# A differential-attention and mixture-of-experts kernel: set-up in a written order, q spread one piece to a round, and the second norm's statistics taken from the first's

## Chip, core and metric

The kernel runs on one core of a Trainium2 chip. The metric is the device time of one execution in microseconds (us). Several executions are timed, and the median counts. A profiled execution has a time of its own, and beside it a span, which goes from the first to the last instruction of the core.

## What is computed

The input x has 8 sequences of 512 tokens with 128 features. Each sequence goes through differential attention with 16 heads of 8 features, a residual and a layer norm, then through a mixture of 8 experts of which each token uses 2, again with a residual and a layer norm.

```python
q, k1, k2, v = (heads(x @ W.T) for W in (Wq, Wk1, Wk2, Wv))
a1 = softmax(causal(q @ k1.T * SCALE))
a2 = softmax(causal(q @ k2.T * SCALE))
attn = a1 - sigmoid(lambda_logit) * a2
attn = attn / max(sum(abs(attn), -1), 1e-6)
x = layernorm(x + (attn @ v) @ Wo.T)

# the experts
xn = (x - mean(x)) * rsqrt(var(x) + EPS) * gamma + beta
probs = softmax(xn @ router_w.T / 1.5)
w, idx = top_k(probs, 2)
y = sum over the two chosen e of w[e] * (silu(xn @ W1[e]) @ W2[e])
x = layernorm(y + x)
```

The first layer norm has no gain and no offset. The experts' own norm, which is called the second norm here, is taken of the first norm's result. All is in float32, with EPS = 1e-5 in each of the three norms.

## The kernel before

**Tiles.** A sequence is worked in 16 units `Unit(b, j)` of 32 queries. A unit holds the scores of 4 heads times 32 queries on the 128 partitions, for 4 groups of heads and 2 softmaxes. Unit j looks at L = 32 (j + 1) keys, so units grow along a sequence. The first 8 units are worked in 2 slots, the last 8 in 4 slots.

**Rounds.** One slot gives one round (`round_of`, from line 1122). All five engines work in the order in which a round writes its instructions (`manual_schedule`, line 1180); nothing reorders them later. A round does, in this order: the products with v of a unit that is ready (line 529, tile po); the next slot's scores on PE (line 366, tile sc, and the mask's product on line 375 from i4 and mk); copies of transposed weights on ACT (line 512, aT); steps that wait in `on_act`; the negated maxima on DVE (lines 388 and 396, nm); the transposes of an earlier piece on PE (line 487, pt); steps that wait in `on_dve`; the combination of the two softmaxes, which is on DVE a sum (line 432, junk) and on POOL the scaling of the second softmax (line 442, et); and the exponentials on ACT (line 406, et). After that it takes one task from each of several queues:

- `misc`: the tasks of a block of 128 tokens (`block_tasks`) and of the next sequence's projections (`projection_tasks`). One task is taken per round.
- `routing`: the choice of experts for a chunk of blocks.
- `moves` and `gathers`: indirect DMAs on POOL's queue (lines 811 and 959), which send rows to the tiles of the experts and fetch results. One is taken per round.
- `experts`: tiles of expert work, at a pace that is worked out when a chunk has been routed.

A task often puts its DVE part into `on_dve`, and that part runs in the next round.

**Blocks.** The tasks of a block are `reciprocals`, `normalise`, `project_out`, `first_norm`, `second_norm`, `turn` and `logits`. The DVE part of `project_out` adds the residual (xa, line 590), takes its statistics (`stats_of`, lines 118 and 119) and has POOL raise the variance to the power -1/2 (`rstd_of`: l_ve on DVE at line 110, l_rs on POOL at line 112). `first_norm` writes x1 (line 600), takes the statistics of x1 in the same way and has POOL work out a second power. `second_norm` writes xh (line 615). There are 32 blocks, so 64 pairs of statistics for these two norms; the last layer norm has another 32.

**Projections.** `project_q` multiplies on PE; its part `spread` copies the result to qs on DVE (line 299) and writes four pieces of qb on POOL one after the other (line 301), each with another column of hms, which selects heads. k goes through ACT to kT (line 315). v goes through DVE to vt (line 323), and 8 DMAs on SP copy parts of it to vr (line 327), which the products with v read for short rows of keys.

**Set-up.** Lines 59 to 275 and the projections of sequence 0 (line 1079) stand outside `manual_schedule`. There the framework's scheduler orders the instructions of each engine. It put slam1 (line 226), i4 and mk (lines 218 and 219) ahead of the copy of the first x (line 292) on DVE; the memsets of all constants first on POOL; and the four fills of the row buffers with zero (line 271) ahead of the copies to vr on SP. ACT issues the loads of wq, wv, slam, gam, bet and rw, and works out slam with a sigmoid (line 225).

The first four chunks (6, 9, 9 and 6 blocks) go to experts by rows that are sent; the last 2 blocks go through all 8 experts.

Of the kernel before, what the change touches and what calls it, by code (L numbers as in the profile page):

```python
# [20 lines left out]
def kernel(  # L21
# [43 lines left out]
    nhalf = const.tile([P, CB], F32, name="nhalf")  # L65
    nc.gpsimd.memset(nhalf, -0.5)
    rank = const.tile([P, CB, E], F32, name="rank")
    for e in range(E):
        nc.gpsimd.memset(rank[:, :, e : e + 1], float(E - e))

# [4 lines left out]
    before = const.tile([P, P], BF16, name="before")  # L75
    nc.gpsimd.memset(before, 1.0)
    nc.gpsimd.affine_select(
        out=before,
        in_=before,
        pattern=[[1, P]],  # L80
        compare_op=ALU.is_ge,
        fill=0.0,
        base=-1,
        channel_multiplier=-1,
    )
    ones = const.tile([P, P], BF16, name="ones")
    nc.gpsimd.memset(ones, 1.0)

    upto = const.tile([P, E, E], F32, name="upto")
    for e in range(E):  # L90
        nc.gpsimd.memset(upto[:, e, : e + 1], 1.0)
        if e + 1 < E:
            nc.gpsimd.memset(upto[:, e, e + 1 :], 0.0)

    fill = const.tile([P, E, CB], F32, name="fill")
    for k in range(CB):
        nc.gpsimd.memset(fill[:, :, k : k + 1], float(P * k))

    def tiles_of(nb):

        return (2 * nb * P + E * (P - 1)) // P

    number = const.tile([P, tiles_of(CB), E], F32, name="number")
    for t in range(tiles_of(CB)):
        nc.gpsimd.memset(number[:, t, :], float(t))

# [27 lines left out]
    with ExitStack() as actx:  # L134
# [52 lines left out]
        for h in range(4):  # L187
            nc.scalar.dma_start(
                slam[Q * h : Q * h + Q, :],
                lam.rearrange("(g h) -> h g", h=4)[h].partition_broadcast(Q),  # L190
            )
        for g in range(NG):
# [3 lines left out]
            )  # L196
        nc.scalar.dma_start(gam, gamma.unsqueeze(1))
        nc.scalar.dma_start(bet, beta.unsqueeze(1))
        nc.scalar.dma_start(rw_sb, rw)


        nc.gpsimd.memset(hsel, 1.0)
        for low in (True, False):
# [9 lines left out]
            )  # L213
        nc.vector.tensor_reduce(hm, hsel, AX.X, ALU.max)
        nc.vector.tensor_scalar_mul(hms, hm, SCALE)
        for g in range(NG):
            r = slice(32 * g, 32 * g + 32)
            nc.vector.tensor_copy(i4[r], identb[r, r].unsqueeze(1).to_broadcast([32, 4, Q]))
            nc.vector.tensor_copy(mk[r], maskb[r, r])
        nc.vector.tensor_copy(wq_sb.rearrange("p (a b d) -> p a b d", a=NP, b=2), wqp[:, :, :, 0:HD])  # L220
        for s in range(2):
            nc.vector.tensor_copy(
                wk_sb[:, s].rearrange("p (a b d) -> p a b d", a=NP, b=2), wkp[:, :, :, s, 0:HD]
            )
        nc.scalar.activation(slam, slam, AF.Sigmoid)
        nc.vector.tensor_scalar(slam1, slam, 1.0, None, ALU.add)
        for h in range(4):
            nc.vector.tensor_scalar_mul(wo_sb[:, h, :], won, hm[:, h : h + 1])


# [29 lines left out]
        zero = aw.tile([P, D], F32, name="zero")  # L260
        nc.gpsimd.memset(zero, 0.0)
        chunks, n0 = [], 0
# [3 lines left out]
        for n0 in range(n0, NB, 2):  # L266
            chunks.append(Chunk(n0, 2, False))

        for c in chunks:
            if c.sparse:  # L270
                nc.sync.dma_start(
                    c.xs.rearrange("(t p) d -> p t d", p=P),
                    zero.unsqueeze(1).to_broadcast([P, c.nt, D]),
                )
        chunk_of = {n: c for c in chunks for n in range(c.n0, c.n0 + c.nb)}

        def projection_tasks(b):
# [16 lines left out]
            def project_q():  # L294
                pm = ps_m.tile([P, T], F32, tag="pm", name=f"pmq_{b}")
                nc.tensor.matmul(pm, lhsT=wq_sb, rhs=xTf, start=True, stop=True)

                def spread():
                    nc.vector.tensor_copy(qs, pm)
                    for h in range(4):  # L300
                        nc.gpsimd.tensor_scalar(  # L301
                            qb[:, :, h, :],
                            qs.rearrange("p (j q) -> p j q", q=Q),
                            hms[:, h : h + 1],
                            1.0,
                            ALU.mult,
                            ALU.mult,
                        )

                on_dve.append(spread)  # L310
# [226 lines left out]
        def block_tasks(b, i, blk):  # L537
# [39 lines left out]
            def project_out():  # L577
# [10 lines left out]
                def residual():  # L588
                    xa = bp.tile([P, D], F32, tag="xa", name=f"xa_{n}")
                    nc.vector.tensor_add(xa, pm, xts[b][:, i, :])  # L590
                    mv = bp.tile([P, 1, 2], F32, tag="mv1", name=f"mv1_{n}")
                    stats_of(bp, xa, mv[:, 0, :], "l1")
                    s["xa"], s["mv"], s["rs"] = xa, mv, rstd_of(bp, mv, 1, "l1")

                on_dve.append(residual)

            def first_norm():
                def norm():
                    x1 = s["x1"] = ch.x1[:, ci, :]
                    nc.vector.tensor_scalar(  # L600
                        x1, s["xa"], s["mv"][:, 0, 0:1], s["rs"], ALU.subtract, ALU.mult
                    )
                    mv = bp.tile([P, 1, 2], F32, tag="mv2", name=f"mv2_{n}")
                    stats_of(bp, x1, mv[:, 0, :], "l2")
                    s["mv2"], s["rs2"] = mv, rstd_of(bp, mv, 1, "l2")

                on_dve.append(norm)

            def second_norm():
                def norm():  # L610
                    if ch.sparse:
                        s["xh"] = ch.xh[:, ci, :]
                    else:
                        s["xh"] = bp.tile([P, D], F32, tag="xh", name=f"xh_{n}")
                    nc.vector.tensor_scalar(
                        s["xh"], s["x1"], s["mv2"][:, 0, 0:1], s["rs2"], ALU.subtract, ALU.mult
                    )

                on_dve.append(norm)
# [16 lines left out]

            return [reciprocals, normalise, project_out, first_norm, second_norm, turn, logits]

# [428 lines left out]

        on_act, on_dve, on_dve_late = [], [], []

# [3 lines left out]
        def run(steps):  # L1073
            now = list(steps)
            steps.clear()
            for step in now:
                step()

        for task in projection_tasks(0):
            task()  # L1080
            run(on_dve)
            run(on_act)

# [38 lines left out]
        def round_of(now=None, ahead=None):  # L1122
# [40 lines left out]
            for _ in range(1 if now else 2):  # L1163
                if moves:
                    moves.popleft()()
                elif gathers and (now or not misc and not routing):
                    gathers.popleft()()
# [12 lines left out]
        with tc.manual_schedule(  # L1180
# [6 lines left out]
            }  # L1187
        ):
            last = None
            for b in range(B):  # L1190
# [21 lines left out]
            while (  # L1212
                to_combine or to_transpose or to_evacuate or to_multiply
                or misc or routing or experts or moves or gathers or on_act or on_dve or on_dve_late
            ):
                round_of()
# [49 lines left out]
```

## Time and profile before

| | |
|---|---|
| Time of three runs | 1224.34, 1222.89 and 1214.82 us, median 1222.89 us |
| Profiled execution | 1229.11 us, span 1227.1 us |
| Mean granted clock of TensorE | 0.923 |
| Busy share of the span | PE 90%, DVE 77%, ACT 64%, POOL 44% |
| First scores on PE | 20.03 us after the span's start |
| Last scores on PE | about 1105 us |

PE is TensorE's matmul, PEld its loading of weights, DVE VectorE, ACT ScalarE, POOL GpSimd and SP SyncE, which here only issues DMAs. Times in the profile's rows count from the span's start, and line numbers are those of the kernel before. A row of the timeline gives start, duration, engine, line, operation, the tile written and the tile read, the shape, the count, and in brackets the idle time of the engine ahead of it with what ended it. A row of the chain of waits gives start, duration and what the chain went through at that time. The row that begins with PEclk shows the clock that TensorE was granted in 40 equal parts of the span, in tenths of full speed.

### The profile page before, as it was taken

The numbers are of one execution on the slowest core, as the hardware profiler recorded it, in microseconds if no ns is written. First come the engines' busy times: TensorE is split into PE (matmuls) and PEld (weight loads), VectorE is DVE, ScalarE is ACT, GpSimd is POOL, SyncE is SP. The second block draws the span as 40 slices with busy tenths as digits, with TensorE's granted clock in tenths as the row PEclk, the third lists the DMA queues.
The fourth block names the chain that finished last, engine by engine and source line by source line (L and its number), as shares of the span: only waits on it lengthen the run. The fifth ranks groups of instructions, "written<-read, shape, count | busy, mean of one in ns | idle before, by whom it ended". The sixth has DMA issues, their size and how long they took to land.

```text
span 1227.1 us, 28291 instructions
## 1 busy us (share of the span) xinstructions
PE 1101.6 (90%) x9450; PEld 779.6 (64%) x9450; DVE 948.4 (77%) x2900; ACT 782.7 (64%) x2776; POOL 543.0 (44%) x967
## 2 busy tenths in 40 slices
PE   4999899888999899989898899988899889997786
PEld 2556555555666666666566666665667667776675
DVE  4688778867888678887689888879767897975656
ACT  4578767557777667766576777776567665763221
POOL 4343434464433343356556442343643762364333
PEclk8699969878999789997899999999989998999998
DMA  8000000011121111110133113221222333435762
GB/s 245 7 8 1 10 2 8 26 59 30 30 82 45 33 42 53 46 41 23 38 99 85 57 45 91 63 56 47 72 78 72 105 107 105 126 92 149 215 188 68
DMA packets 128897, 84.30 MB, mean 69 GB/s; under 512 B 22896, under 2 KB 114288, under 8 KB 128752
## 3 DMA queue, kind: packets, MB, share of 16 engines
q1 hardware_dynamic: 110944, 68.25, 19.8%
q0 software_dynamic: 3840, 7.87, 2.3%
q10 hardware_dynamic: 13968, 6.37, 1.8%
q8 instruction: 76, 1.25, 0.4%
q14 instruction: 69, 0.57, 0.1%
HBM read 63.31 MB, written 17.56 MB: 66 GB/s over the span
## 4 chain that ended last, share of the span: by engine, by line
PE 56%; DVE 19%; ACT 10%; issue 6%; POOL 4%; DMA 4%; ACTq 0%; SPq 0%; POOLq 0%; DVEq 0%
PE pt L487 18%; PE sc L366 12%; ACT et L406 6%; PE po L529 5%; PE sc_None L366 5%; PE pa L914 5%; PE pz L934 4%; DVE junk L432 3%; DVE nm L396 3%; DVE nm L388 2%; PE pmo L580 2%; ACT aT L512 2%; DVE l_st L118 1%; DMA got<-ys,row 1%; POOL qb L301 1%
## 5 line engine op out<-in xcount | busy, mean ns | idle before, releaser
L442 POOL TENSOR_SCALAR et<-et,c 128x224 f32<-128x224 f32 (+15 forms) x512 | 266.9, 526 | 438.6 <-DVE junk L432 301.2
L487 PE MATMUL pt<-ident,et 128*128 128x128 f32 (+1 forms) x2048 | 330.0, 297 | 36.6 <-POOL et L442 20.7
L406 ACT ACTIVATE et<-sc,nm 128x512 f32<-128x512 f32 (+7 forms) x512 | 299.7, 593 | 68.8 <-DVE nm L396 46.8
L487 PEld LDWEIGHTS pt<-ident,et 128*128 128x128 f32 (+1 forms) x2048 | 231.9, 146 | 171.6 <-issue 59.9
L396 DVE TENSOR_REDUCE nm<-sc 128x2 f32<-128x576 f32 (+7 forms) x256 | 251.6, 983 | 41.8 <-PE sc L375 41.5
L432 DVE SCALAR_TENSOR_TENSOR junk<-et,c 128x224 f32<-128x224 f32 (+15 forms) x512 | 264.2, 516 | 9.6
L512 ACT COPY aT<-pt 128x384 f32<-128x384 f32 (+5 forms) x488 | 185.8, 407 | 130.5 <-PE pt L487 127.4
L366 PE MATMUL sc<-kT,qb 32*128 32x384 f32 (+7 forms) x1024 | 246.5, 558 | 13.3 <-ACT et L406 12.4
L406 ACT ACTIVATE et<-sc_None,nm 128x256 f32<-128x256 f32 (+7 forms) x512 | 188.1, 385 | 31.2 <-DVE nm L388 23.2
L366 PE MATMUL sc_None<-kT,qb 32*128 32x512 f32 (+7 forms) x512 | 118.6, 546 | 22.3 <-ACT et L406 21.1
L388 DVE TENSOR_REDUCE nm<-sc_None 128x4 f32<-128x256 f32 (+7 forms) x128 | 96.0, 751 | 40.8 <-PE sc_None L375 40.5
L366 PEld LDWEIGHTS sc<-kT,qb 32*128 32x128 f32 x1024 | 78.4, 187 | 63.7 <-ACT et L406 30.6
L112 POOL TENSOR_TENSOR l_rs<-l_ve,nhalf 128x1 f32<-128x1 f32 x96 | 62.5, 651 | 124.9 <-DVE l_ve L110 102.8
L934 PE MATMUL pz<-xgT,w 128*128 128x128 f32 x704 | 101.5, 291 | 11.4 <-DVE xgT L908 10.7
L406 ACT ACTIVATION_READ_ACCUMULATOR et<-sc_None,nm 128x1 f32 x512 | 107.4, 210 | 0.0
L406 ACT ACTIVATION_READ_ACCUMULATOR et<-sc,nm 128x1 f32 x512 | 103.2, 202 | 0.0
L934 PEld LDWEIGHTS pz<-xgT,w 128*128 128x128 f32 x704 | 92.0, 203 | 16.7 <-DVE xgT L908 13.5
L914 PE MATMUL pa<-w,hT 128*128 128x128 f32 x704 | 100.0, 289 | 0.6 <-ACT ysb L924 0.6
L914 PEld LDWEIGHTS pa<-w,hT 128*128 128x128 f32 x704 | 93.2, 206 | 1.9 <-issue 1.2
L879 ACT ACTIVATE th<-pz 128x512 f32<-128x512 f32 x88 | 52.7, 599 | 58.3 <-PE pz L934 52.1
L529 PE MATMUL po<-aT,vt 128*32 128x128 f32 (+1 forms) x2048 | 85.2, 291 | 0.0
L811 POOL DMA_INDIRECT xs<-xh,row x60 | 65.4, 1089 | 42.9 <-DMA xs<-xh,row 30.8
(148 smaller groups left out, 1316.2 us busy)
## 6 DMA issues: line engine op xcount, KB each, us to landing
w<-in_w_dram SPq DMA_DIRECT2D x192, 256.0 KB, 3.0
xg<-xs SPq DMA_DIRECT2D x88, 64.0 KB, 3.3
ys<-ysb ACTq DMA_DIRECT2D x88, 64.0 KB, 1.5
xs<-zero SPq DMA_DIRECT2D x2, 1600.0 KB, 13.8
xs<-zero SPq DMA_DIRECT2D x2, 1216.0 KB
xt<-in_x_dram SPq DMA_DIRECT2D x8, 256.0 KB
out_dram<-ot SPq DMA_DIRECT2D x32, 64.0 KB, 2.1
vr<-vt SPq DMA_DIRECT2D x32, 32.0 KB, 1.9
```

The costliest lines, as they stand in the source:

```text
L366: nc.tensor.matmul(parts[gi][:, :, :L], lhsT=qb[r, j].rearrange("p h q -> p (h q)"), rhs=kT[r, sets, :L], start=True, stop=False,)
L388: nc.vector.tensor_reduce(self.nm[:, g, :], sc.rearrange("p g (s l) -> p g s l", s=2)[:, :, :, : self.L], AX.X, ALU.max, negate=True,)
L396: nc.vector.tensor_reduce(self.nm[:, g, s], sc[:, :, : self.L], AX.X, ALU.max, negate=True)
L406: nc.scalar.activation(self.et[:, g, si, : self.L], sc[:, gi, lo : lo + self.L], AF.Exp, bias=self.nm[:, g, si : si + 1], accum_out=self.b ...
L432: nc.vector.scalar_tensor_tensor(junk[:, :L], self.et[:, g, 1, :L], self.c2[:, g : g + 1], self.et[:, g, 0, :L], ALU.mult, ALU.max, accum_ ...
L442: nc.gpsimd.tensor_scalar(self.et[:, g, 1, :L], self.et[:, g, 1, :L], self.c2[:, g : g + 1], -1.0, ALU.mult, ALU.mult,)
L487: nc.tensor.matmul(pt[: len(gs) * kw, x_, :], lhsT=lhsT, rhs=ident, is_transpose=True, start=(k == 0), stop=(k == 1),)
L512: nc.scalar.copy(self.aT[: rows[done], self.used + done : self.used + end, :], pt[: rows[done], done:end, :],)
L529: nc.tensor.matmul(self.blk["po"][32 * g : 32 * g + 32, self.jj, :], lhsT=v[:rows, kb, 32 * g : 32 * g + 32], rhs=self.aT[:rows, self.at[g ...
L811: nc.gpsimd.indirect_dma_start(ch.xs[:, :], bass.IndirectOffsetOnAxis(ap=ch.row[:, k, c : c + 1], axis=0), ch.xh[:, c, :], None,)
L914: nc.tensor.matmul(pm[:, 1, :], lhsT=hT[y][:, f, :], rhs=w[y][1][:, f, :], start=(f == 0), stop=(f == NF - 1),)
L934: nc.tensor.matmul(pz[:, f, :], lhsT=w[t][0][:, f * P : (f + 1) * P], rhs=xgT[t], start=True, stop=True,)
```

## The change

**Set-up.** The projections of sequence 0 and the set-up steps that are no load now stand inside `manual_schedule`, in a written order: first x's transposes and their copy, then hm and hms, then the other projections with the spreads of q, then i4 and mk, slam, slam1 and wo_sb, then the constants on POOL, and at the end the four zero fills. The loads of slam, gam, bet and rw go from ACT to SP. The sigmoid is worked out as 0.5 (tanh(x / 2) + 1), with the tanh on ACT.

**Spreads.** The four pieces of qb go into a queue `on_pool`, and a round takes one of them, in place of a task of `moves` or `gathers`. In set-up all four run at once.

**Second norm.** With v the variance of the residual sum, the first norm's result has mean 0 and variance v / (v + EPS). So the second norm of it is the residual sum, less its mean, times ((1 + EPS) v + EPS²)^(-1/2). `norms` takes the place of `first_norm` and `second_norm`: both powers come from one POOL instruction on two columns, and xh and x1 are written from xa in one step.

```diff
+                    ve = bp.tile([P, 2], F32, tag="l1_ve", name=f"l1_ve_{n}")
+                    nc.vector.tensor_scalar(ve[:, 0:1], mv[:, 0, 1:2], EPS, None, ALU.add)
+                    nc.vector.tensor_scalar(
+                        ve[:, 1:2], mv[:, 0, 1:2], 1.0 + EPS, EPS * EPS, ALU.mult, ALU.add
+                    )
+                    rs = bp.tile([P, 2], F32, tag="l1_rs", name=f"l1_rs_{n}")
+                    nc.gpsimd.tensor_tensor(rs, ve, nhalf[:, :2], ALU.pow)
...
-            def first_norm():
+            def norms():
                 def norm():
-                    x1 = s["x1"] = ch.x1[:, ci, :]
-                    nc.vector.tensor_scalar(
-                        x1, s["xa"], s["mv"][:, 0, 0:1], s["rs"], ALU.subtract, ALU.mult
-                    )
-                    mv = bp.tile([P, 1, 2], F32, tag="mv2", name=f"mv2_{n}")
-                    stats_of(bp, x1, mv[:, 0, :], "l2")
-                    s["mv2"], s["rs2"] = mv, rstd_of(bp, mv, 1, "l2")
-
-                on_dve.append(norm)
-
-            def second_norm():
-                def norm():
+                    x1 = ch.x1[:, ci, :]
...
-                    nc.vector.tensor_scalar(
-                        s["xh"], s["x1"], s["mv2"][:, 0, 0:1], s["rs2"], ALU.subtract, ALU.mult
-                    )
+                    for k, dst in enumerate((s["xh"], x1)):
+                        nc.vector.tensor_scalar(
+                            dst,
+                            s["xa"],
+                            s["mv"][:, 0, 0:1],
+                            s["rs"][:, 1 - k : 2 - k],
+                            ALU.subtract,
+                            ALU.mult,
+                        )
...
                 def spread():
                     nc.vector.tensor_copy(qs, pm)
-                    for h in range(4):
...
+                    on_pool.extend(lambda h=h: spread_head(h) for h in range(4))
...
             for _ in range(1 if now else 2):
-                if moves:
+                if on_pool:
+                    on_pool.popleft()()
+                elif moves:
                     moves.popleft()()
...
+            first = projection_tasks(0)
+            first.pop(0)()
+            run(on_dve)
+            nc.vector.tensor_reduce(hm, hsel, AX.X, ALU.max)
+            nc.vector.tensor_scalar_mul(hms, hm, SCALE)
+            for task in first:
+                task()
+                run(on_dve)
+                run(on_act)
+                run(on_pool)
+
+            for g in range(NG):
+                r = slice(32 * g, 32 * g + 32)
+                nc.vector.tensor_copy(i4[r], identb[r, r].unsqueeze(1).to_broadcast([32, 4, Q]))
+                nc.vector.tensor_copy(mk[r], maskb[r, r])
+
+            nc.scalar.activation(slam, slam, AF.Tanh, scale=0.5)
+            nc.vector.tensor_scalar(slam, slam, 1.0, 0.5, ALU.add, ALU.mult)
+            nc.vector.tensor_scalar(slam1, slam, 1.0, None, ALU.add)
+            for h in range(4):
+                nc.vector.tensor_scalar_mul(wo_sb[:, h, :], won, hm[:, h : h + 1])
+            nc.gpsimd.memset(zero, 0.0)
+            for e in range(E):
+                nc.gpsimd.memset(rank[:, :, e : e + 1], float(E - e))
...
+            for c in chunks:
+                if c.sparse:
+                    nc.sync.dma_start(
+                        c.xs.rearrange("(t p) d -> p t d", p=P),
+                        zero.unsqueeze(1).to_broadcast([P, c.nt, D]),
+                    )
```

## The prediction

> **What bounds the kernel now.** I read the page first: busy shares, the clock row, the chain that ended last.
>
> ```profile
> PE 1101.6 (90%) x9450; PEld 779.6 (64%) x9450; DVE 948.4 (77%) x2900; ACT 782.7 (64%) x2776; POOL 543.0 (44%) x967
> PEclk8699969878999789997899999999989998999998
> PE 56%; DVE 19%; ACT 10%; issue 6%; POOL 4%; DMA 4%; ACTq 0%; SPq 0%; POOLq 0%; DVEq 0%
> ```
>
> No engine is the bound alone. The chain changes between PE, DVE and ACT within every round, because a round hands a score tile from PE to DVE to ACT to DVE to POOL and back to PE. So an instruction that goes is worth what stood on the chain, not its busy time. In the clock row the digits 6 to 8 are stretches at half clock. Next I read the start in the chain of waits (start us, duration us, what):
>
> ```profile
> 7.22 3.20 DMA slam<-in_lam_dram
> 10.49 1.28 ACT L225
> 12.03 0.17 DVE slam L226
> ...
> 13.63 0.70 DVE xT L292
> ...
> 17.28 2.71 POOL qb L301 x4
> ...
> 20.54 0.30 DVE nm L388
> 20.86 3.17 ACT et L406 x22
> 24.03 7.56 DMA vr<-vt
> 31.63 1.21 PE po L529 x8
> ```
>
> Two detours are to be seen. DVE copied xT only at 13.63, behind slam's load and sigmoid and eight small copies, although its input pmx was there at 6.78 (5.69 + 1.09, timeline). And the first po waited until 31.63 for vr, whose DMAs stood on SP behind four zero fills; PE was idle 2.1 us for it (group row of po<-aT,vr: 2.1 <-DMA vr<-vt).
>
> Then the timeline where POOL spreads q of the next sequence, four in a row (start, duration, engine, what, idle before):
>
> ```profile
> 72.32 0.61 DVE L422 TENSOR_TENSOR c<-c,r 128x4 f32<-128x4 f32 x1
> 72.96 0.93 DVE L432 SCALAR_TENSOR_TENSOR junk<-et,c 128x288 f32<-128x288 f32 x1
> 74.56 0.86 DVE L432 SCALAR_TENSOR_TENSOR junk<-et,c 128x288 f32<-128x288 f32 x1
> 76.09 0.50 DVE L432 SCALAR_TENSOR_TENSOR junk<-et,c 128x288 f32<-128x288 f32 x1
> 72.23 2.89 POOL L301 TENSOR_SCALAR qb<-qs,hms 128x512 f32<-128x512 f32 x4 [0.62 <-DVE c L418]
> 75.85 0.55 PE L487 MATMUL pt<-ident,et 128*128 128x128 f32 x3 [1.20 <-POOL et L442]
> ```
>
> While POOL spreads, et waits behind it and PE stands 1.20 us. And DVE's operations with two tensors are longer: junk 0.93 and 0.86 against 0.50 right after, c 0.61 against 0.16.
>
> **Part 1, set-up order.** I lay the after order on the old times. wk lands at 7.20 and its two copies end at 7.59 as before; xT is then first on DVE, at 7.6 instead of 13.63, 6.0 us sooner, with hm and hms after it (0.34, beside PE's q product). From xT's start to the last spread it took 6.35 us (13.63 to 19.98) and to the end of the vt copy 6.76 (20.39). So qb is there at about 13.95 and vt at 14.4. But what was ahead of xT now stands between vt and the first nm: eight i4 and mk copies (0.78 + 0.70), two on slam (2 x 0.17), four wo_sb (0.88), 2.7 us. The first nm starts at 17.1 instead of 20.54: 3.4 us gained. Bounds: 0 (a load is late) and 6.0 (nothing of the 2.7 counts).
>
> Loads: SP now issues xt and wk (0.45 + 0.49), slam (4 x 0.39), won (4 x 0.64), gam, bet and rw (0.44 + 0.46 + 0.34), 7 us in all. One of won's waits for wk's landing (7.20), so SP is through at about 10; slam, at 3.2 us to landing, is there by 7 to 10, won by 12. They are needed at 13.3 (tanh behind kT's copies) and 16.2 (wo_sb). If won came 2 us later than 16.2, those 2 us would be lost. ACT's second table load (1.28 us from 19.32) ended at 20.60, before nm was done at 20.84: nothing. On POOL the constants' memsets (2.9 us, 1.82 to 4.84 without the mask, and zero) go behind the spreads, 13.95 to 16.9; et is first wanted at 24.00 - 3.4 = 20.6, so 3.7 us of cover.
>
> vr: eight issues at 0.62 us (median of the line) from 14.4 end at 19.4, and 1.9 us to landing gives 21.3; po will want it at 29.5 (end of the pt before it) - 3.4 = 26.1. The stall of 2.1 us goes (bounds 0 and 2.1). The zero fills, 14.75 us of issue, follow until about 34 and hold up only xt of sequence 1 on SP, wanted at 68.74; the filled rows are first written at 230.4.
>
> Part 1 sums to 5.5 us.
>
> **Part 2, spreads.** The same seven spreads outside set-up (28 instructions) stay; they stand one to a round, behind that round's et. PE's waits for et behind the bursts, read at each of the seven: 1.20, 1.19, 0.30, 0, 3.53, 0, 0.99, together 7.2 us. Against it: DVE's stretched operations stay possible. Per burst they cost 0.45 + 0.43 + 0.36 = 1.24 us, 8.7 over seven. A spread of 0.69 that starts behind an et of 0.50 ends 1.19 us after the junk that released it; DVE's nm between takes 0.81, so the next junk can lose 0.38, four times a sequence: 28 x 0.4 = 11 us. Gain 7.2 + 8.7 - 11 = 4.9 if all counts, minus 2.5 if PE's waits are filled otherwise, 11.2 if nothing is lost (the spreads' own time on the chain between 60 and 1110, summed from its pieces). I take 4, near the first, as other waits are known to come up behind. The scatters wait up to four rounds behind spreads; the two built programs have the same PE work after the last scores (375 instructions in both), so this moves nothing into the tail.
>
> On this the Trainium skill speaks against the change: "SBUF — State Buffer", section "Who interferes with whom", says that VectorE with two SBUF inputs and a GpSimd instruction reading SBUF exclude each other, the later one waiting until the first ends. The rows above (0.93 for 0.50) fit. By the rule's full wait of one 0.69 spread each, 28 x 0.69 = 19 us would be lost and part 2 would cost 3 us; by the row it gains 4.
>
> **Part 3, norms.** One block, from the timeline:
>
> ```profile
> 60.65 0.33 DVE L600 TENSOR_SCALAR x<-xa,mv,l_rs 128x128 f32<-128x128 f32 x1
> 61.02 0.29 DVE L118 BATCH_NORM_STATS2 l_st<-x 128x6 f32<-128x128 f32 x1
> 61.35 0.18 DVE L119 BATCH_NORM_AGGREGATE mv<-l_st 128x2 f32<-128x6 f32 x1
> 61.56 0.15 DVE L110 TENSOR_SCALAR l_ve<-mv 128x1 f32<-128x1 f32 x1
> 61.80 0.69 POOL L112 TENSOR_TENSOR l_rs<-l_ve,nhalf 128x1 f32<-128x1 f32 x1 [1.47 <-DVE l_ve L110]
> ```
>
> The second statistics go: 0.29 + 0.18 of DVE and one pow on POOL for each of 32 blocks. l_ve stays twice (the second moves into the first round), both normalisations stay but share a round. With the gaps that is (0.33 + 0.21) = 0.54 us, 17 us of DVE at most. x of line 600 stands on the chain for 16 of 32 blocks, so 16 x 0.5 = 8 us stood there; behind it another engine is soon late (ACT 64% and PE 90% busy), so I take 5, bounds 0 and 17. The pow with two columns has no row; one column takes 0.547 to 0.947 here, so two cost between that and double, which is no more than the two pows of before. POOL loses up to 32 x 0.57 = 18 us of work, and l_rs is on the chain for 1.8 us between 60 and 1110: 1 us. Every block's logits come one round sooner; the last block's end at 1139 while the sparse tiles keep PE until 1183, so that hides it.
>
> **Sum.** 5.5 + 4 + 5 + 1 = 15.5 us. The profiled execution took 1229.1 (span 1227.1 and 2.0 around it), giving 1213.6; it lies 6.2 above the median of 1222.9. Taken off the median: 1207.4. The chance bounds are 1% of the median, 1210.7 and 1235.1, about what a measurement here can tell from no change.
>
> **Rivals.**
> *Only the start counts.* DVE and POOL savings hide behind PE (90% busy), as POOL's 302 us of waiting for junk suggests; against it stand the measured PE waits behind the bursts. 1222.9 - 5.5 = 1217.4.
>
> *The clock helps too.* The first half-clock stretch lasts from about 24.5 to 55; PE was fully busy from 32, after the vr wait, and got the clock back some 21 us later. Another stretch (152 to 176) also lasts 20.5 us at full business. If the count starts anew at an idle gap, removing the wait ends the stretch some 5 to 10 us sooner, 3 to 5 us of work; with part 3 at 10: 1207.4 - 4 - 5 = 1198. The Trainium skill's "TensorE: Matmul & The Clock Gate", section "What's actually happening", has the clock return after about 3.4 us of business; the trace's 21 us contradicts it, and by the rule nothing would come on top.
>
> *The clock hurts (slower).* At the start of sequences the matmuls are short and PE falls to half clock:
>
> ```profile
> 152.00:176.00 24.00, 23.00 (x125) 13.43 (x126) 16.90 (x62) 16.30 (x72) 8.27 (x19) 0.57 0.00 1
> 690.00:714.00 24.00, 20.77 (x183) 14.30 (x181) 21.53 (x78) 18.72 (x80) 10.46 (x23) 1.00 0.20 58
> ```
>
> The column after POOL is the clock. DVE did 16.9 us of work in 24 instead of 26.1 in 30 at full clock (60 to 90), so such a stretch costs 24 - 16.9 x 30 / 26.1 = 4.6 us. The starts of later sequences, as at 690, escape it now. To end over 1% slower it needs (12.2 + 15.5) / 4.6 = 6 new stretches; with seven, 1207.4 + 32 = 1240. For it: a one-round shift moves every boundary. Against: late sequences are filled with expert matmuls.
>
> **How the numbers follow.** Forecast 0.50, only the start 0.27, clock helps 0.15, clock hurts 0.08. About 0.45 of the forecast's 0.50 lies below 1210.7: faster 0.45 + 0.15 = 0.60; slower 0.08; the rest 0.32 within 1%. Low is 1222.9 - (8.1 + 11 + 9) = 1195; high is 1222.9 - 2.1 = 1221, which leaves out the clock rival and the ends of the first.
>
> **What would show it.** First nm near 17 us; no DMA wait ahead of the first po; waits of pt for et above 1 us after spreads gone; DVE busy near 933 (948.4 less 32 x 0.477); 64 pows; same number of half-clock stretches. It is wrong if nm starts after 20, if junk beside spreads grows by more than 11 us in all, or if PE's share on the chain takes over all that DVE gives up.

## The result, and the profile after

The changed kernel takes 1217.05 us (median of 20 runs), the kernel before in the same runs 1224.12 us: ratio 0.9932, 95% interval 0.9908 to 0.9956. The gain is 7 us, less than half of the 15.5 that were forecast; the time lies in the stated range. Its profiled execution took 1212.04 us, with a span of 1210.1 and a mean granted clock of 0.927.

The page after (busy shares, clock row, chain):

```profile
PE 1093.9 (90%) x9450; PEld 776.2 (64%) x9450; DVE 927.1 (77%) x2837; ACT 780.4 (64%) x2775; POOL 526.8 (44%) x935
PEclk7699969797999999989998999997899799998998
PE 60%; DVE 16%; ACT 11%; issue 6%; POOL 4%; DMA 3%; ACTq 1%; POOLq 0%; SPq 0%; DVEq 0%
```

DVE lost 21.3 us of work and POOL 16.2, and the chain moved from DVE (19% to 16%) to PE (56% to 60%).

The chain of waits at the start:

```profile
7.64 0.61 DVE xT L251
...
14.38 0.70 DVE vt L284
15.16 1.95 DMA vr<-vt
17.11 0.08 issue
17.19 0.19 DVE i L1165
...
18.18 0.88 DVE wo_sb L1172 x4
19.06 0.21 DVE nm L349
...
28.27 0.59 PE po L490 x8
```

xT stands at 7.64, as forecast, and no DMA stands right ahead of po. (The row that names vr's DMA from 15.16 covers time in which DVE stood in two copies, as the next rows show.) But nm starts at 18.97 (timeline; 17.1 forecast). DVE's timeline shows what took the difference:

```profile
14.38 0.69 DVE L284 COPY vt<-pmv 128x512 f32<-128x512 f32 x1 [3.28 <-PE pmv L281]
14.99 1.85 DVE L1165 COPY i<-identb 32x128 bf16<-32x128 bf16 x1
15.09 1.76 DVE L1166 COPY mk<-maskb 32x32 bf16<-32x32 bf16 x1
16.89 0.18 DVE L1165 COPY i<-identb 32x128 bf16<-32x128 bf16 x1
```

The first pair of copies took ten times as long as the others. POOL's memsets of the constants ran from 13.86 to 16.79, one after the other; the copies end when they do.

POOL at the first spreads outside set-up, in the timeline:

```profile
71.21 0.51 POOL L403 TENSOR_SCALAR et<-et,c 128x288 f32<-128x288 f32 x1 [1.05 <-DVE junk L393]
71.70 0.97 POOL L258 TENSOR_SCALAR qb<-qs,hms 128x512 f32<-128x512 f32 x1
72.64 0.50 POOL L403 TENSOR_SCALAR et<-et,c 128x288 f32<-128x288 f32 x1
73.12 0.69 POOL L258 TENSOR_SCALAR qb<-qs,hms 128x512 f32<-128x512 f32 x1
```

Each spread stands behind an et. PE's waits of pt for et fell from 20.7 to 9.7 us (first line before, second after, from PE's waits: total, times, longest):

```profile
PE pt L487 <- POOL et L442: 20.7, 24, 3.5
```

```profile
PE pt L448 <- POOL et L403: 9.7, 17, 1.6
```

So all three parts do in the profile what they should, and yet more than half of the forecast gain is missing.

**The clock.** Runs of one and the same kernel spread widely (those of the kernel before by 29 us within one set of runs, 1211.4 to 1240.4), and the spread follows the mean granted clock of each run: over 199 runs (the kernel before and the first twelve experiments) a run with 0.01 less clock takes 6.6 us more. So each kernel below has three numbers: its median; its mean clock less that of the kernel before; and its difference *at equal clock*, from straight lines of time over clock with a common slope (5.6 to 8.0 us per 0.01, by the set) and an offset for each kernel. The last is an adjustment, since the clock was not set by hand, but it splits what a part saves from what it does to the clock. A clock difference from 12 runs is known to 0.004 or 0.005. Runs more than 1.5% above their kernel's fastest are left out of means and ratios.

### The profile page after: what moved, and what is told of

It reads as the page before. It is cut to its first block, busy times and chain, and to the rows that moved or that the text cites. A ratio compares the mean times of both kernels' runs of the same rounds, so it can differ in the third digit from the quotient of the medians.

```text
span 1210.1 us, 28192 instructions
## 1 busy us (share of the span) xinstructions
PE 1093.9 (90%) x9450; PEld 776.2 (64%) x9450; DVE 927.1 (77%) x2837; ACT 780.4 (64%) x2775; POOL 526.8 (44%) x935
## 4 chain that ended last, share of the span: by engine, by line
PE 60%; DVE 16%; ACT 11%; issue 6%; POOL 4%; DMA 3%; ACTq 1%; POOLq 0%; SPq 0%; DVEq 0%
PE pt L448 19%; PE sc L327 13%; ACT et L367 7%; PE po L490 5%; PE pz L900 5%; PE pa L880 5%; PE sc_None L327 5%; DVE junk L393 2%; DVE nm L357 2%; PE pmo L541 2%; ACT aT L473 2%; DVE nm L349 2%; POOL et L403 1%; DVE hT L847 1%; POOL xs L777 1%
## 5 line engine op out<-in xcount | busy, mean ns | idle before, releaser
L403 POOL TENSOR_SCALAR et<-et,c 128x224 f32<-128x224 f32 (+15 forms) x512 | 270.9, 534 | 458.1 <-DVE junk L393 295.0
L448 PE MATMUL pt<-ident,et 128*128 128x128 f32 (+1 forms) x2048 | 326.7, 296 | 26.8 <-ACT aT L473 14.9
L393 DVE SCALAR_TENSOR_TENSOR junk<-et,c 128x224 f32<-128x224 f32 (+15 forms) x512 | 258.6, 505 | 9.6
L847 DVE SCALAR_TENSOR_TENSOR hT<-th,pz 128x512 f32<-128x512 f32 x88 | 60.2, 684 | 30.8 <-ACT th L845 30.6
```

The source lines that it names most:

```text
L393: nc.vector.scalar_tensor_tensor(junk[:, :L], self.et[:, g, 1, :L], self.c2[:, g : g + 1], self.et[:, g, 0, :L], ALU.mult, ALU.max, accum_ ...
L403: nc.gpsimd.tensor_scalar(self.et[:, g, 1, :L], self.et[:, g, 1, :L], self.c2[:, g : g + 1], -1.0, ALU.mult, ALU.mult,)
L448: nc.tensor.matmul(pt[: len(gs) * kw, x_, :], lhsT=lhsT, rhs=ident, is_transpose=True, start=(k == 0), stop=(k == 1),)
```

## The experiments

| Run | What it is | Median (before) us | Ratio, 95% interval | Clock | At equal clock us |
|---|---|---|---|---|---|
| e1 | set-up alone | 1217.06 (1224.44) | 0.9926 [0.9893, 0.9958] | +0.0035 | -5.3 ± 1.5 |
| e2 | norms alone | 1213.49 (1224.44) | 0.9903 [0.9875, 0.9931] | +0.0066 | -7.5 ± 1.6 |
| e3 | spreads alone | 1225.03 (1224.44) | 1.0012 [0.9982, 1.0043] | -0.0102 | -4.6 ± 1.6 |
| e5 | changed kernel, constants early | 1218.31 (1224.44) | 0.9900 [0.9859, 0.9941] | -0.0090 | -15.4 ± 2.0 |
| e8 | changed kernel again | 1220.37 (1223.61) | 0.9975 [0.9937, 1.0013] | -0.0115 | -12.8 ± 1.9 |
| e9 | changed kernel, spreads in a burst | 1212.56 (1223.61) | 0.9916 [0.9880, 0.9951] | -0.0031 | -12.4 ± 1.6 |
| e6 | e5 with its start ordered again | 1207.41 (1223.61) | 0.9868 [0.9816, 0.9920] | +0.0009 | -15.1 ± 2.0 |
| e13 | e6 once more | 1215.87 (1225.12) | 0.9944 [0.9914, 0.9975] | -0.0084 | -12.8 ± 2.7 |
| e10 | e6, spreads in a burst | 1210.19 (1225.12) | 0.9894 [0.9846, 0.9942] | +0.0005 | -13.3 ± 3.1 |
| e12 | e6 with the old norms | 1218.78 (1225.12) | 0.9962 [0.9929, 0.9995] | -0.0079 | -9.9 ± 2.7 |
| e7 | e3, scatters not put back | 1222.87 (1223.61) | 1.0001 [0.9958, 1.0044] | -0.0085 | -6.1 ± 1.7 |
| e11 | e3 and the burst as well | 1232.73 (1225.12) | 1.0064 [1.0025, 1.0103] | -0.0050 | +3.9 ± 2.6 |
| e14 | before, no spreads from the third sequence on | 1222.07 (1223.64) | 0.9959 [0.9919, 0.9999] | -0.0026 | -7.1 ± 1.6 |
| e15 | e3, two spreads to a round | 1223.17 (1223.64) | 0.9996 [0.9961, 1.0032] | -0.0089 | -7.8 ± 1.7 |
| e16 | before, each burst twice | 1261.92 (1223.64) | 1.0318 [1.0272, 1.0364] | -0.0180 | +26.3 ± 2.5 |
| e17 | e3, single spread ahead of et | 1223.78 (1224.41) | 0.9949 [0.9906, 0.9992] | -0.0016 | -6.8 ± 1.9 |
| e18 | e3, the four in one round, behind et | 1223.02 (1224.41) | 0.9999 [0.9965, 1.0032] | -0.0042 | -4.1 ± 1.5 |

e5, e6, e10 and e16 have 6 runs, the others 12. e17's ratio, clock and time at equal clock rest on six of its twelve runs; over all twelve its clock was 0.9243 against 0.9316 before. e14 leaves out part of the computation, so its time is that of less work.

**The parts one by one.** e1, e2 and e3 are the kernel before with one part of the diff each. e5 is the changed kernel with POOL's constants written ahead of `projection_tasks(0)`:

```diff
             nc.vector.tensor_scalar_mul(hms, hm, SCALE)
+            nc.gpsimd.memset(zero, 0.0)
+            for e in range(E):
+                nc.gpsimd.memset(rank[:, :, e : e + 1], float(E - e))
...
             for task in first:
...
                 nc.vector.tensor_scalar_mul(wo_sb[:, h, :], won, hm[:, h : h + 1])
-            nc.gpsimd.memset(zero, 0.0)
-            for e in range(E):
-                nc.gpsimd.memset(rank[:, :, e : e + 1], float(E - e))
...
```

> The kernel before with the set-up part alone (order, loads, tanh); spreads in a row and both norms' statistics as before. Theory A (the start was mis-sized by a collision of DVE's small copies with POOL's memsets, and much of the other two parts hides behind PE): first nm at 19.0 us and the first po without a DMA wait as in the changed kernel, a lead of 3 us at the start of the second sequence, time 3 us below before. Theory B (all three parts are worth what the prediction gave them, but the changed start makes PE fall to half clock some 8 us sooner, and that gives 7 us back): the half-clock stretch begins near 16 us instead of 24, and the time is equal to before or up to 3 us above it.

> The kernel before with the second norm's statistics derived from the first's, and nothing else. Both theories have 32 pairs of statistics and 32 powers less and DVE's busy time about 15 us lower. Theory A: most of it hides behind PE, 2 to 4 us below before. Theory B: 6 us below before, as the prediction had it.

> The kernel before with the spreads of q one to a round, and nothing else. Both theories have no junk longer than its kind by more than 0.1 us beside a spread and no wait of pt for et above 1 us after a spread. Theory A: PE makes up for the wait in the rounds behind it, 1 to 3 us below before. Theory B: 4 us or more below.

> The changed kernel with POOL's memsets of the constants written ahead of the spreads instead of behind them; POOL is idle there from 4.4 to 11.2 us. If the memsets hold up DVE's first i4 and mk copies (1.85 and 1.76 us where the next ones take 0.18), all eight take 0.2 us or less and the first nm starts at 17.2 instead of 19.0 us; the time is 1 to 2 us below the changed kernel's, so 9 to 10 below before. The rival, that the two copies are long for another reason (they wait for code, or for the vt copy ahead), leaves them above 1 us and nm at 19.

Neither theory held: e1 and e2 gained more than both gave them, and e3 gained nothing. In e5 POOL has no memset beside the copies of i4 and mk, and they are short:

```profile
5.29 2.06 DVE L192 COPY wq_sb<-stage 128x128 f32<-128x128 f32 x1 [5.29 <-DMA stage<-in_wq_dram]
...
15.52 0.17 DVE L1188 COPY i<-identb 32x128 bf16<-32x128 bf16 x1
15.62 0.15 DVE L1189 COPY mk<-maskb 32x32 bf16<-32x32 bf16 x1
```

nm then starts at 17.88 instead of 18.97, so the memsets were the cause of the long copies. The copy of wq, which now stands beside them, takes 2.06 us, to 7.35, where POOL's series ends at 7.28; in the kernel before it took 0.48. But 1.1 us is a small share of what is missing. The parts at equal clock are 5.3 + 7.5 + 4.6 = 17.4 us if they add, more than the forecast's 15.5. What stood out was that the spreads alone gained 4.6 us at equal clock and nothing in time: their clock was lower by 0.010, which costs 6.6 us.

**Do the single spreads lower the clock?** e9 takes only them back out of the changed kernel; e7 is e3 with a round that may issue a spread and a scatter; e6 is e5 with i4, mk and lambda's steps ahead of the projections and the wo products in `misc`.

```diff
# e9
-                    on_pool.extend(lambda h=h: spread_head(h) for h in range(4))
+                    for h in range(4):
+                        nc.gpsimd.tensor_scalar(
...
# e7
                 if on_pool:
                     on_pool.popleft()()
-                elif moves:
+                if moves:
# e6: the loop over first now stands behind these lines
             nc.scalar.activation(slam, slam, AF.Tanh, scale=0.5)
             nc.vector.tensor_scalar(slam, slam, 1.0, 0.5, ALU.add, ALU.mult)
             nc.vector.tensor_scalar(slam1, slam, 1.0, None, ALU.add)
+            for task in first:
...
-            for h in range(4):
-                nc.vector.tensor_scalar_mul(wo_sb[:, h, :], won, hm[:, h : h + 1])
+            def outputs_by_head():
+                for h in range(4):
+                    nc.vector.tensor_scalar_mul(wo_sb[:, h, :], won, hm[:, h : h + 1])
+
+            misc.append(outputs_by_head)
```

> The changed kernel once more, so that its granted clock and that of the kernel before are compared on one chip with the next three. Theory A' (the three parts simply do not add, some of the gain is taken twice): its clock equals that of the kernel before within .003 and its time at equal clock is about 7 us below. Theory C (the parts add up to some 17 us at equal clock, and spreading q one piece to a round costs granted clock): its mean clock is lower than that of the kernel before by .005 to .010, its raw gain 6 to 10 us and its gain at equal clock 12 to 17 us.

> The changed kernel with the four spreads of q issued in a burst again; the set-up and the norms stay changed. Theory A' (the parts do not add): within 3 us of the changed kernel, some 1215 to 1219. Theory C (the single spreads cost clock): the clock goes up to .935 or more, the gain at equal clock is 5.3 + 7.5 = 12.8 us, and the time lies near 1207, 8 to 10 us below the changed kernel: it would beat both.

> The changed kernel with its start ordered again: the constants of POOL early, the mask copies and lambda's tanh ahead of the first projections' copies, the wo products deferred to the list of small tasks; spreads single. First nm at 15.1 instead of 18.97 us. If a start earlier by 3.9 us comes through to the end at equal clock, some 4 us below the changed kernel at equal clock; theory C says that its clock stays as low as the changed kernel's, since the spreads are the same.

> The spreads alone (set-up and norms as before), but a round that issues a spread issues a scatter as well, so that no scatter is put back by a round. If the lower clock of the spreads alone (.9198 against .9300) came from scatters, and so experts, that start later, the clock goes back to .928 or more and the time to 1219 to 1221. If it comes from the single spreads themselves (a TensorE without its pause at each sequence's start), the clock stays near .920 and the time near 1225.

The changed kernel fell to -0.0115 of clock again; with the burst back (e9) it is -0.0031 (0.9306, short of the 0.935 that was expected), and its median is 7.8 us lower. So the spreads cost time in it. Later scatters are not the reason (e7: -0.0085). e6 spoke against: single spreads, and the clock of before. Its first nm came at 16.12, held by lambda's load, and not at 15.1. The next set repeated it (e13) beside its relatives: e10 is e6 with e9's edit, e12 is e6 with `first_norm` and `second_norm` as before, and e11 is e3 with the burst ahead of the queue.

```diff
# e11
+                    for h in range(4):
+                        spread_head(h)
                     on_pool.extend(lambda h=h: spread_head(h) for h in range(4))
```

> The kernel with the start ordered again (e6), but with the four spreads of q in a burst, as before. Theory C (single spreads cost some .010 of granted clock wherever they stand, and e6's .9347 was luck): clock .945, at equal clock 12 to 15 us below the kernel before, time 1200 to 1204. Theory D (single spreads cost clock only together with the starts that had them so far: the clock depends on where the work falls against the throttle, and the start moves that): clock .930 to .935, within 3 us of the repeat of e6 in this call.

> The kernel with the start ordered again, once more, beside its three relatives on one chip. Theory C: its clock falls to .922 to .926 and its time to 1213 to 1217, since it has the single spreads. Theory D: the clock stays within .003 of the kernel before and the time at 1207 to 1210.

> The spreads alone, single (set-up and norms as before), but with the burst of four issued as well, ahead of them: q is spread twice, the second time for nothing. TensorE's pause at a sequence's start is back and POOL has 28 spreads more, 19.6 us of its time. If the lost pause is what lowered the clock to .9198, the clock goes back to .928 to .932; at equal clock it is then at most 2 us from the kernel before, so some 1222 to 1227. If the clock falls by the single spreads themselves, it stays at .918 to .922 and the time goes to 1228 to 1234.

> The kernel with the start ordered again and single spreads, but with both norms as before. Theory C: clock .920 to .925 and a time of 1218 to 1222. Theory D: as in e6 the clock is within .004 of the kernel before, and the time is 7.5 us (the norms' worth at equal clock) above e6's, 1214 to 1217.

The repeat, e13, had -0.0084 and 1215.87 us: e6's six runs did not stand for the kernel. With the burst (e10) the same start has +0.0005 and 1210.19. Over the kernel before and these twelve experiments, a fit has one effect for each part and an offset for each set of runs; e5's early constants, the start of e6 and its relatives, and e11's second spreading have an effect of their own (95% intervals):

| Part | Time us | Clock | At equal clock us |
|---|---|---|---|
| set-up | -3.0 ± 2.3 | -0.0020 ± 0.0028 | -4.4 ± 1.3 |
| norms | -6.2 ± 2.0 | +0.0010 ± 0.0025 | -5.5 ± 1.1 |
| single spreads | +3.6 ± 1.8 | -0.0102 ± 0.0023 | -3.2 ± 1.2 |

**Do the parts add?** The table takes it that they do. With one more term, for the new norms and the single spreads together, the same fit says that they do not: at equal clock the norms alone give 7.2 ± 1.2 us, the single spreads alone 4.8 ± 1.3, and the two together 4.5 ± 1.7 less than their sum (in time 4.0 ± 3.2 less). The traces show a saving that was counted twice. PE's waits of pt for et during a burst and in the 6 us behind it sum to 7.2 us in the kernel before and to 6.2 in e1, but only to 0.7, 1.3 and 1.2 in e2, e9 and e10, which have the bursts and the new norms. The longest of them, in the kernel before and in e2:

```profile
597.15 0.55 PE L487 MATMUL pt<-ident,et 128*128 128x128 f32 x3 [3.53 <-POOL et L442]
```

```profile
581.56 0.55 PE L487 MATMUL pt<-ident,et 128*128 128x128 f32 x3 [0.68 <-POOL et L442]
```

So beside the new norms the single spreads have next to nothing left to save. Why a burst falls better there was not tested; a block then has one task less in `misc`, so the rounds are filled in another way.

**Why is their clock lower?** The texts on record ask whether PE's pauses keep the clock up. (They put the bursts at the sequences' starts; they stand some 50 to 70 us behind them.) e11 has the burst ahead of the single spreads; its clock lay between. e2, e9 and e10 speak against it: their bursts leave PE next to no pause, and they keep the clock (+0.0066, -0.0031, +0.0005). The next runs double the pause, and take it away:

```diff
# e16: each burst twice
-                    for h in range(4):
+                    for h in (0, 1, 2, 3, 0, 1, 2, 3):
# e14: two buffers of qb, spread for the first two sequences alone
-                    for h in range(4):
+                    for h in range(4 if b < 2 else 0):
# e15: e3, two to a round
                 if on_pool:
                     on_pool.popleft()()
+                    on_pool.popleft()()
```

> The kernel before without any spreads from the third sequence on: q's heads are spread for the first two sequences alone, and the later ones use those (part of the computation is left out, so its time is that of less work). POOL has 24 instructions fewer, TensorE's waits behind the bursts go, and nothing is issued one to a round. If the lost pauses lower the clock: clock .918 to .924, gain at equal clock 4 to 9 us, time within 3 us of the kernel before. If the single spreads themselves lower it (their place, not the pause that is gone): clock as before within .004 and time 1215 to 1219.

> The spreads alone (set-up and norms as before), two to a round. POOL is then held for 1.4 us at a time, and TensorE's pauses for et come back in part. If the pauses keep the clock up: clock about half way, .923 to .928. If it is the spreading over rounds: two rounds instead of four, also about half way; so this run only tells whether there is a steady passage (half way) or a step (.920 or .932).

> The kernel before with each burst issued twice, eight spreads in a row, the second four for nothing. POOL is held for 5.6 us at a time and TensorE's pauses at the sequences' starts become longer by 2.8 us or less each. If pauses keep the clock up, it rises above that of the kernel before, .936 to .942, and at equal clock the kernel is 15 to 22 us slower (7 x 2.8 us and the stretched operations). If pauses have nothing to do with it, the clock stays within .004.

Pauses do the reverse: e16's clock fell by 0.018. Its timeline on PE, and its busy time in stretches of 8 us (PE, PEld, DVE, ACT, POOL, then the clock):

```profile
81.23 0.90 PE L487 MATMUL pt<-ident,et 128*128 128x128 f32 x3 [4.06 <-POOL et L442]
```

```profile
72.00:80.00 8.00, 5.14 (x39) 2.10 (x37) 7.30 (x18) 4.35 (x15) 5.86 (x8) 1.00 0.01 2
80.00:88.00 8.00, 6.77 (x25) 4.31 (x25) 0.82 (x1) 3.39 (x11) 2.13 (x5) 0.51 0.00 0
88.00:96.00 8.00, 8.00 (x36) 5.76 (x36) 4.39 (x11) 3.01 (x10) 1.43 (x3) 0.50 0.15 26
96.00:104.00 8.00, 7.91 (x74) 5.02 (x73) 7.62 (x25) 4.64 (x16) 4.09 (x8) 0.92 0.01 3
```

The clock falls in the gap of 4.06 us and stays halved for some 17 us, with a full PE from 81.23 on. e14 bounds the part from above: with nearly all spreads gone the gain is 7.1 us at equal clock, and most of the clock stays (-0.0026 ± 0.005; the time of 1219 at most that was expected with it did not come). So a lost pause is not the cause; it lies with the spreads being single, in a way that these runs do not show. The last two change the place alone and the number alone:

```diff
# e17: e3, each spread ahead of its round's et
             run(on_dve)
+            if on_pool:
+                on_pool.popleft()()
...
-                if on_pool:
-                    on_pool.popleft()()
-                elif moves:
+                if moves:
# e18: e3, all four behind one round's et
                 if on_pool:
-                    on_pool.popleft()()
+                    run(on_pool)
```

> The spreads alone (set-up and norms as before), one to a round, but each ahead of its round's et, where the burst stood. If the place behind et is what lowers the clock, the clock goes back to .928 or more; if it is that they are single, it stays at .918 to .925. At equal clock some 0 to 5 us below the kernel before, since every et of four rounds now waits up to 0.69 us.

> The spreads alone, all four in one round as before, but behind that round's et, where the single ones stood. If the place behind et lowers the clock, it stays at .918 to .925; if it is that they are single, the clock goes back to .928 or more. The next round's et waits for up to 2.8 us: at equal clock within 4 us of the kernel before.

Four in one round behind et keep more of the clock (-0.0042) than one or two to a round (e3, e7, e15: -0.0102, -0.0085, -0.0089), which points to the number; e17 depends on which of its runs are counted and says nothing. The intervals of ± 0.004 overlap, so this stays open.

## Why the prediction was right or wrong

**Part 2 is the step that failed**, in two ways. It put the spreads at +4 us: 7.2 of PE's waits and 8.7 of stretched DVE operations against 11 lost again. The 7.2 were read in the kernel before and added to part 3 as if the two had nothing to do with each other. But part 3 alone takes these waits away: with the new norms the bursts cost PE 0.7 to 1.3 us. So at equal clock the part gives 4.8 ± 1.3 us where it stands alone, near the forecast, and 4.5 ± 1.7 less beside the new norms. The 11 us did not come: the DVE operations with two tensors that overlap a spread ran, in all, 5.8 us over the median of their kind in the kernel before, 3.4 in e3 and 1.5 in the changed kernel; nor did the 19 us of the other price that the prediction names. The second way is a term that was left at nothing: the total was made at the clock of before, and the single spreads lower it by 0.0102 ± 0.0023. At 6.6 us per 0.01 that is 6.7 us. By the table the part costs 3.6 ± 1.8 us in time; the 4 us forecast and the 3.6 lost make up 7.6 of the 8.4 us that were missing. Which stretches at half clock come on top could not be read: ten profiles with single spreads have 162 to 193 us at half clock, and seven with a burst or no later spreads (e11 and e16 aside) 137 to 191. Why single spreads lower the clock stays open.

**Part 1** was 5.5, measured 4.4 ± 1.3 at equal clock and 3.0 ± 2.3 in time. One term was mis-sized: the first nm moved by 1.57 us and not 3.4. Of the 1.9 us that are missing, 0.7 came ahead of the copies (vt's copy ended at 15.07, not 14.4) and 1.2 in them: the eight copies were priced by their old rows, without POOL beside them. The plan put POOL's memsets under cover of et's late start; what they ran beside was DVE's copies. The Trainium skill, "SBUF — State Buffer", section "Who interferes with whom", says that a copy may enter a mode that takes the port pair shared with GpSimd, and that the later of two then waits for the whole other instruction. The row agrees and goes further: the copy lasted until the end of a whole series of memsets, 1.85 us against 0.18. The vr wait went, as forecast.

**Part 3** was 6, measured 5.5 ± 1.1 at equal clock by the table and 7.2 ± 1.2 where it stands without the single spreads. The pow with two columns took 0.73 us on average, where one column took 0.59: within the bounds.

What the norms do to the clock can be read in one place. PE before, in the timeline, where the second norm's statistics were on DVE:

```profile
418.95 0.33 PE L623 MATMUL pmn<-ident,xh 128*128 128x128 f32 x1 [0.23 <-DVE xh L615]
420.40 1.65 PE L366 MATMUL sc_None<-kT,qb 32*128 32x384 f32 x4 [1.11 <-ACT et L406]
```

and the stretches of 8 us there:

```profile
412.00:420.00 8.00, 6.62 (x62) 4.29 (x60) 7.32 (x34) 5.90 (x31) 3.66 (x10) 1.00 0.36 108
420.00:428.00 8.00, 7.60 (x37) 5.04 (x38) 4.72 (x19) 4.55 (x21) 2.29 (x6) 0.51 0.03 9
428.00:436.00 8.00, 8.00 (x38) 4.58 (x37) 5.51 (x18) 5.06 (x20) 3.24 (x7) 0.50 0.01 3
```

The same work in the changed kernel:

```profile
407.75 0.27 PE L589 MATMUL pmn<-ident,xh 128*128 128x128 f32 x1
...
410.60 0.92 PE L327 MATMUL sc_None<-kT,qb 32*128 32x384 f32 x4 [0.48 <-ACT et L367]
```

```profile
404.00:412.00 8.00, 6.60 (x62) 4.04 (x61) 7.58 (x35) 6.69 (x33) 3.38 (x9) 1.00 0.36 107
412.00:420.00 8.00, 7.28 (x65) 4.70 (x64) 6.70 (x26) 6.30 (x27) 3.53 (x9) 1.00 0.12 22
420.00:428.00 8.00, 7.09 (x65) 5.05 (x63) 7.26 (x21) 6.70 (x27) 4.09 (x9) 1.00 0.21 64
```

With the old norms PE stands 1.11 us and falls to half clock for 17 us; with the new ones the stop is 0.48 and the clock stays. In the profiles ten of the eleven kernels with the old norms have 17 us at half clock there (e16 has 3), and of the eight profiles with the new norms six have none, one 3 and one 7. Such a stretch is 0.007 of the mean clock (17 x 0.5 / 1220), as much as e2 gained; over all kernels the norms show only 0.0010 ± 0.0025, so the gain of this place is not kept as a whole, and where it goes was not found.

**The rivals.** "Only the start counts" gave 1217.4, next to the measured 1217.05, by luck: its reason is refuted, as the norms gain 6.2 ± 2.0 and the start 3.0 ± 2.3. "The clock helps too" did not come: the first stretch at half clock lasted 37.5 us (16.4 to 53.9) where it had lasted 30.7 (24.2 to 54.9), without the vr wait. "The clock hurts" had the right kind of mechanism and the wrong size and place: not new stretches at each later sequence's start, but 0.010 on the mean. The forecast treated the clock as a rival beside the sum, where it belongs into each term.

**The marks that were named.** DVE's busy time is 927 (933 forecast), 64 pows, no DMA ahead of po, no wait of pt above 1 us behind a spread: these held, and nearly so the number of stretches at half clock, 17 where there were 19. nm at 17 did not. One sign of being wrong came: PE's share of the chain rose by at least what DVE's lost (56% to 60%, 19% to 16%).

## To carry to other kernels

Before savings are added, see whether one part removes the wait that another is to save. Where a clock falls after short stops of PE, price an edit twice: by what it saves, and by the stops that it makes or removes, each of which can cost several times its length. With such a clock compare many runs, note the clock of each, and try each part of a change alone; here a kernel without the single spreads (e9, 0.9916) beats both the kernel before and the changed kernel of the same set (e8, 0.9975). Before work is moved on POOL, look at what DVE does at that time.

## What the hardware showed unexpectedly

- The clock changes on a grid of 3.41 us, and short stops are enough for a fall. In the 19 traces all 645 changes of the clock lie within 0.02 us of a grid of 3.41 us, whose place differs from trace to trace; so the stretches at half clock last 3.4 us or multiples of it, up to 37.5 us. Of 5783 windows of this grid at full clock, none of the 4384 in which PE idled under 0.6 us was followed by half clock, but 59 of 782 with 0.6 to 1.0 us, 101 of 320 with 1.0 to 1.5 and 173 of 297 above. By this the same stop can cost or not, as it falls in the grid; that this makes the runs of one kernel spread is an inference, as no run moved the grid alone.
- A full PE does not always bring the clock back. Of the 806 windows at half clock in which PE idled under 0.2 us, all 103 without matmuls on 32-row weights (the scores and the mask, `32*128` in the rows) were followed by full clock, and none of the 389 with 1.5 us or more of them. The prediction's two stretches of some 21 us at full business are of this kind, with 1.0 to 2.5 us of such matmuls in each window. The Trainium skill, "TensorE: Matmul & The Clock Gate", section "What's actually happening", has the clock fall after an idle window of about 3.4 us and come back after a busy one. The length of the window agrees with the grid; but by the rule the stop of 1.11 us above would have cost nothing, and the scores show that a busy window is not enough. The traces decide.
- A POOL series of memsets held a DVE copy of 0.18 us for 1.85 us, and in e5 one of 0.48 us for 2.06 us.
- Twice the burst cost 26 us at equal clock, for 19.6 us of POOL work, where 15 to 22 were expected; its clock, expected to rise or stay, fell by 0.018.
